# Layer 3 of a four-layer convolution stack: ScalarE's copy of a block moved ahead of the work of the block before it

## The chip, the cores and the metric

The kernel runs on one NeuronCore of a Trainium2 chip. The time is the device time of one launch in microseconds, told as the median of several runs. A profile is one more execution, with its own time. PE is TensorE (matrix products into PSUM), ACT is ScalarE, DVE is VectorE, POOL is GpSimd, SP issues DMAs. Each engine works through its own queue in order; semaphores join them.

## The reference

The input x is 8 images of 128 channels, 56 x 56, float32. Four layers follow, each x = x + f(groupnorm(x)): a window attention, a recurrent network over the pixels, a mixed 3x3 and 1x1 convolution, and, as layer 3, a residual block of two 3x3 convolutions. The change is all in layer 3:

```python
def _L3_conv_ref(x, w1, w2, gamma1, beta1, mean1, var1, gamma2, beta2, mean2, var2):
    residual = x
    out = _conv3x3(x, w1, stride=1)
    out = jax.nn.relu(_bn(out, gamma1, beta1, mean1, var1))
    out = _conv3x3(out, w2, stride=1)
    out = _bn(out, gamma2, beta2, mean2, var2)
    return jax.nn.relu(out + residual)
...
x = x + _L3_conv_ref(_gn(x), ...)
```

## The kernel before

Channels lie on the 128 partitions; X holds all images in SBUF. In layer 3 each 3x3 convolution is computed along the rows in a transformed form: four output pixels of a row come from six sums of the input pixels, multiplied by six transformed weight columns, times three row offsets. An image is cut into 4 blocks of 14 rows (RB = 14, H4 = 14 groups of four pixels in a row, 196 positions). Per image there are two phases: blocks pc3a_0 to pc3a_3 (called a_0 to a_3 here) for the first convolution, reading va, and pc3b_0 to pc3b_3 (b_0 to b_3) for the second, reading vb.

The steps of a block:

- products() (L1440): 18 matrix products on TensorE, 36 records in the profile, into three PSUM banks, m[0], m[1], m[2]. There are six banks, so two blocks can be open. A bank is free again once its readers are done.
- outputs(): ACT copies m[0] to SBUF as c (L1452). DVE makes the sum s and difference d of c and m[1] (L1453, L1454), then w and two rows of the result y (L1456 to L1459), then, after what `between` puts there, the other two rows with m[2] (L1461). s, d, w and y have one buffer each, c two.
- a phase: six() (L1302, L1304, L1305) on ACT applies the batch norm and relu and writes y into `edge`, six planes with the neighbours at the row ends. column_sums() turns `edge` into the sums of vb in three parts: outer() on POOL (ce at L1415, fg at L1416), inner() on DVE (ab at L1420, two planes at L1421 and L1422), ends() on DVE (four planes, L1426 to L1428).
- b phase: ACT applies the second batch norm to y, giving u (L1540). Then normal3() on ACT normalizes a block of the next image into `pad` (L1302 to L1305 again, through six()), and column_sums() makes its sums of va; here POOL does L1421 and L1422 of inner(). residual() on DVE adds the normalized and the raw x (L1553, L1554), and SP issues the store of the block (L1555). u has two buffers.

The order on PE, ACT, DVE and POOL is the order of the program text, set by hand. Two lists hold work for a later place: `middle` is run between the rows of y of the next block, `waiting` after its y. In the kernel before, a block is in ACT's queue: copy, then six() or u and normal3() of this same block; then comes the copy of the next block. In the b phase DVE's place for inner() of the next image is `between`; ends() and then the residual come after y.

A block b_i needs the rows of vb that a_i and a_(i+1) make, since the third row offset reaches two rows into the next block; a_i needs va of blocks up to i only. The first image has more in it: statistics and norm of the seven other images (stats3(), Rest), and va made at its beginning (into_va with "begin").

Of the kernel before, what the change touches and what calls it, by code (L numbers as in the profile page):

```python
# [10 lines left out]
F32 = mybir.dt.float32  # L11
I32 = mybir.dt.int32
U32 = mybir.dt.uint32
AF = mybir.ActivationFunctionType
# [30 lines left out]
def conv_stack_kernel(ctx: ExitStack, tc: tile.TileContext, a: dict, out: bass.AP):  # L45
# [1027 lines left out]
    def convolutions(held=None):  # L1073

        with ExitStack() as l2:
# [246 lines left out]
            with ExitStack() as order:  # L1322
                if held is not None:
                    order.enter_context(tc.manual_schedule(engines={ET.PE, ET.Activation, ET.DVE, ET.Pool}))
                for i in range(NBLK):
                    norms[0].stats(i)
                warm(8, ps_g, "pg")
                norms[0].mean_mm()
                norms[0].mean_end()
                norms[0].var_mm()  # L1330
                warm(26, ps_g, "pg")
                norms[1].stats(0)
                norms[0].root()
                for c in range(5):
                    norms[0].normal([c])
                    spread(0, c)
                nc.vector.tensor_mul(w1, w1, m1)
                nc.vector.tensor_reduce(bsum, bmat, AX.X, ALU.add)
                for i in range(1, NBLK):
                    norms[1].stats(i)  # L1340
                for n in range(B * NBLK):
                    b, i = divmod(n, NBLK)
                    if i == 0 and b + 2 <= B:
                        norms.append(Norm((b + 2) % B, f"l2_{b + 2}"))
                    then = norms[b + 1]
# [36 lines left out]
                    if i == 0 and b in (1, 3):  # L1382
                        weights.append(transformed(f"w{(b + 1) // 2}c_t"))
                    if 1 <= b <= 4 and i >= 3:
                        for f in weights[-1][1][i - 3 + 4 * ((b - 1) % 2) :][:1]:
                            f()
# [56 lines left out]
                            )  # L1443
                return pc

            def outputs(m, name, between):

                shape = [P, 2, RB * H4]
                c, s, d, w = (
                    blk.tile(shape, F32, name=f"{k}_{name}", tag=k, bufs=1 + (k == "c")) for k in ("c", "s", "d", "w")  # L1450
                )
                nc.scalar.copy(c, m[0])  # L1452
                nc.vector.tensor_tensor(s, c, m[1], ALU.add)  # L1453
# [7 lines left out]
                nc.vector.tensor_tensor(at[:, 0:4:3], w, m[2], ALU.add)  # L1461
                return at
# [26 lines left out]

            waiting, middle = [], []

            def settle(fs):
                for f in fs:
                    f()
                fs.clear()

            def layer3(b, begin):  # L1500
                more = b + 1 < B
                rest = Rest() if b == 0 else None
                for i in range(NB):
                    name = f"pc3a_{b}_{i}"
                    pc = products(ua, va, i, name)
                    if rest and i == 2:
                        rest.mean_mm()
                    if rest and i == 3:
                        rest.var_mm()
                    if i in begin:  # L1510
                        settle(middle)
                        settle(waiting)
                        begin[i]()
                    y = outputs(pc, name, lambda: settle(middle))
                    mid = edges[i % 2]
                    six(mid, y, AF.Relu, bn[0][1], bn[0][0])
                    settle(waiting)
                    outer, inner, ends = column_sums(vb, 1 + i * RB, mid, name)
                    outer()
                    middle.append(inner)  # L1520
                    waiting.append(ends)
                    if rest:
                        for k in {0: range(4), 1: range(4, NBLK)}.get(i, ()):
                            stats3(B - 1, k)
                        if i == 2:
                            rest.mean_end()
                        if i == 3:
                            rest.root()
                for i in range(NB):
                    name = f"pc3b_{b}_{i}"  # L1530
                    pc = products(ub, vb, i, name)
                    if i == 0:

                        ends = waiting.pop()
                        settle(waiting)
                        settle(middle)
                        middle.append(ends)
                    y = outputs(pc, name, lambda: settle(middle))
                    u = blk.tile([P, RB * H4, 4], F32, name=f"u_{name}", tag="u")
                    nc.scalar.activation(  # L1540
                        u, y.rearrange("p k x -> p x k"), AF.Identity, bias=shs[:, b : b + 1], scale=bn[1][0]
                    )
                    settle(waiting)
                    if more:
                        normal3(b + 1, i)
                        outer, inner, ends = into_va(f"va_{b}", i, nc.gpsimd)
                        outer()
                        middle.append(inner)
                        waiting.append(ends)
                    flat, cols = u.rearrange("p x k -> p (x k)"), slice(i * RB * HW, (i + 1) * RB * HW)  # L1550

                    def residual(flat=flat, cols=cols):
                        nc.vector.scalar_tensor_tensor(flat, X[:, b, cols], rs[:, b : b + 1], flat, ALU.mult, ALU.add)  # L1553
                        nc.vector.scalar_tensor_tensor(flat, flat, 0.0, X[:, b, cols], ALU.max, ALU.add)  # L1554
                        nc.sync.dma_start(out[b][:, cols], flat)  # L1555

                    waiting.append(residual)

            with ExitStack() as order:
                if held is not None:  # L1560
                    order.enter_context(tc.manual_schedule(engines={ET.PE, ET.Activation, ET.DVE, ET.Pool}))
                for k in range(2):
                    for f in into_va("begin", k, nc.vector, True):
                        f()
                    normal3(0, k + 2)
                begin = {k - 2: lambda k=k: [f() for f in into_va("begin", k)] for k in (2, 3)}
                for b in range(B):
                    layer3(b, {} if b else begin)
                settle(waiting)

    convolutions(held)

# [226 lines left out]
```

## Time and profile before

| | |
|---|---|
| median of the runs | 3569.07 us (3568.85 to 3573.68, three runs) |
| the profiled execution's time | 3572.46 us |
| its span, first to last instruction | 3570.7 us |
| mean granted TensorE clock | 0.985 |
| PE busy | 3421.3 us (96%) |
| DVE busy | 1909.5 us (53%) |
| ACT busy | 1770.0 us (50%) |
| POOL busy | 1393.5 us (39%) |
| layer 3, from its first matrix product at 3073.17 us to the end | 497.5 us |
| one image of layer 3 | 61.2 us |

Shares over the whole span say little here, since the four layers have different limits; layer 3 is the last seventh. A line of the timeline gives start, duration, engine, line, operation, output and inputs with their sizes, and in brackets how long the engine had been idle and what released it. Neighbouring instructions of one engine overlap a little at their ends, so a chain is summed by their starts. A windows row gives the length of the stretch and each engine's busy time in it with its number of instructions, then the granted clock and the DMA share.

### The profile page before, as it was taken

The numbers are of one execution on the slowest core, as the hardware profiler recorded it, in microseconds if no ns is written. First come the engines' busy times: TensorE is split into PE (matmuls) and PEld (weight loads), VectorE is DVE, ScalarE is ACT, GpSimd is POOL, SyncE is SP. The second block draws the span as 40 slices with busy tenths as digits, with TensorE's granted clock in tenths as the row PEclk, the third lists the DMA queues.
The fourth block names the chain that finished last, engine by engine and source line by source line (L and its number), as shares of the span: only waits on it lengthen the run. The fifth ranks groups of instructions, "written<-read, shape, count | busy, mean of one in ns | idle before, by whom it ended". The sixth has DMA issues, their size and how long they took to land.

```text
span 3570.7 us, 87785 instructions
## 1 busy us (share of the span) xinstructions
PE 3421.3 (96%) x30960; PEld 2827.2 (79%) x30960; DVE 1909.5 (53%) x4105; ACT 1770.0 (50%) x5321; POOL 1393.5 (39%) x3774
## 2 busy tenths in 40 slices
PE   8999999999999989999999999999999999988887
PEld 5666666666666669999999999999999943688886
DVE  6888888888787663222111111111122257787787
ACT  5888888888788872222222222222211144454544
POOL 4777777777766651111111111111000056333332
PEclk9999999999999999999999999999999999999999
DMA  5444444444444431111000000000012156100000
GB/s 147 125 123 120 120 125 116 123 116 124 112 112 111 115 89 57 47 45 48 1 1 1 1 1 1 1 1 1 1 51 60 54 144 180 44 32 24 32 23 38
DMA packets 197663, 238.19 MB, mean 67 GB/s; under 512 B 42736, under 2 KB 150128, under 8 KB 197216
## 3 DMA queue, kind: packets, MB, share of 16 engines
q0 software_dynamic: 34624, 117.03, 12.4%
q1 hardware_dynamic: 161760, 115.12, 11.6%
q8 instruction: 250, 4.10, 0.5%
q14 instruction: 197, 1.61, 0.2%
q10 hardware_dynamic: 832, 0.33, 0.0%
HBM read 133.80 MB, written 67.56 MB: 56 GB/s over the span
## 4 chain that ended last, share of the span: by engine, by line
PE 71%; DVE 12%; ACT 6%; issue 6%; DMA 3%; POOL 1%; SPq 1%; POOLq 0%; ACTq 0%; DVEq 0%
PE ps L968 33%; PE pt L539 7%; PE po L1003 5%; PE s L504 5%; PE pc L1194 4%; PE plep L410 4%; PE po L566 3%; PE pi L943 2%; DMA vs<-vpix 2%; DVE nmax L512 2%; ACT e L516 2%; ACT pad L1302 1%; PE pc L1202 1%; PE pvt L296 1%; PE pc3a L1440 1%
## 5 line engine op out<-in xcount | busy, mean ns | idle before, releaser
L968 PE MATMUL ps<-hs,w_gates 128*128 128x136 f32 x7680 | 932.9, 280 | 0.4 <-DVE gk L980 0.4
L968 PEld LDWEIGHTS ps<-hs,w_gates 128*128 128x128 f32 x7680 | 911.1, 190 | 8.6 <-issue 0.6
L516 ACT ACTIVATE e<-s,nmax 128x256 f32<-128x256 f32 x1568 | 728.3, 483 | 199.1 <-DVE nmax L512 199.0
L991 ACT ACTIVATE hs<-ps,bg 128x136 f32<-128x136 f32 x744 | 237.4, 370 | 933.5 <-PE ps L968 926.0
L946 DVE SCALAR_TENSOR_TENSOR inp<-pi,bine,th 128x272 f32<-128x272 f32 x186 | 84.7, 497 | 888.7 <-ACT th L945 888.7
L512 DVE TENSOR_REDUCE nmax<-s 128x2 f32<-128x512 f32 x784 | 507.5, 681 | 43.2 <-PE s L504 42.6
L539 PEld LDWEIGHTS pt<-ident,e 128*128 128x128 f32 x3136 | 352.0, 142 | 130.0 <-issue 50.3
L539 PE MATMUL pt<-ident,e 128*128 128x128 f32 x3136 | 433.7, 281 | 5.4 <-ACT e L516 3.7
L932 POOL TENSOR_TENSOR xn<-X,ctr 128x136 f32<-128x136 f32 (+1 forms) x186 | 96.3, 536 | 875.3 <-PE pi L943 871.3
L968 PEld LDWEIGHTS ps<-inp,w_gates 128*128 128x128 f32 x2976 | 370.2, 190 | 13.5 <-PE pi L943 1.1
L968 PE MATMUL ps<-inp,w_gates 128*128 128x136 f32 x2976 | 375.3, 279 | 0.7 <-DVE inp L946 0.7
L544 DVE COPY eT<-pt 128x512 f32<-128x512 f32 x392 | 267.5, 682 | 149.7 <-PE pt L539 149.7
L516 ACT ACTIVATION_READ_ACCUMULATOR e<-s,nmax 128x1 f32 x1568 | 331.5, 211 | 0.0
L474 POOL COPY ks<-kT 128x64 f32 x1568 | 297.5, 233 | 26.9 <-ACT vrow L302 23.6
L527 POOL TENSOR_TENSOR rc<-rden,own 128x128 f32<-128x128 f32 x392 | 147.7, 396 | 353.0 <-DVE rden L524 199.2
L1440 PE MATMUL pc3a<-va,u_w1c_t 128*128 128x196 f32 x1152 | 217.5, 352 | 39.3 <-ACT c_pc3b L1452 18.6
L566 PE MATMUL po<-eT,vs 128*32 128x128 f32 x6272 | 224.5, 277 | 27.7 <-DMA vs<-vpix 18.1
L544 ACT COPY eT<-pt 128x512 f32<-128x512 f32 x392 | 231.4, 590 | 37.6 <-PE pt L539 37.3
L1440 PEld LDWEIGHTS pc3a<-va,u_w1c_t 128*128 128x128 f32 x1152 | 209.5, 205 | 47.5 <-POOL ce_va L1415 37.9
L504 PE MATMUL s<-ks,qm 32*128 32x256 f32 x3136 | 246.1, 403 | 0.0
L566 PEld LDWEIGHTS po<-eT,vs 128*32 128x32 f32 x6272 | 160.3, 109 | 98.8 <-issue 49.8
L1440 PE MATMUL pc3b<-vb,u_w2c_t 128*128 128x196 f32 x1152 | 202.5, 336 | 21.9 <-DVE vb L1421 14.7
(283 smaller groups left out, 4690.0 us busy)
## 6 DMA issues: line engine op xcount, KB each, us to landing
vs<-vpix SPq DMA_DIRECT2D x1568, 32.0 KB, 2.8
v<-vimg POOLq DMA_DIRECT2D x56, 290.0 KB, 4.1
v<-vimg POOLq DMA_DIRECT2D x56, 289.5 KB, 5.0
v<-vimg POOLq DMA_DIRECT2D x56, 289.0 KB, 5.9
kept<-gk SPq DMA_DIRECT2D x56, 272.0 KB, 2.1
g<-kept SPq DMA_DIRECT2D x56, 272.0 KB, 2.7
xkeep<-X POOLq DMA_DIRECT2D x56, 224.0 KB, 2.4
out_dram<-u_pc3b SPq DMA_DIRECT2D x32, 392.0 KB, 2.4
```

Source lines behind the costliest of these rows:

```text
L474: nc.gpsimd.tensor_copy(kw[:, t : t + 1, :], ks[b][:, bass.ds(at, 1), :])
L504: nc.tensor.matmul(s_["s"][g][:, o, :], w["qm"][h].rearrange("p h x -> p (h x)"), w["kw"][h], start=True, stop=True,)
L512: nc.vector.tensor_reduce(s_["nmax"][:, g, :], s_["s"][g], AX.X, ALU.max, negate=True)
L516: nc.scalar.activation(wins[2 * p + o]["e"][:, g, :], s_["s"][g][:, o, :], AF.Exp, bias=s_["nmax"][:, g, o : o + 1], accum_out=s_["den"][: ...
L527: nc.gpsimd.tensor_tensor(pairs[p]["r"][:, o], rden[:, o].rearrange("p (g c) -> p g c", c=1).broadcast_to((P, 4, CL)), own.rearrange("p (g ...
L539: nc.tensor.transpose(s_["pt"][c][:, g, :], s_["e"][:, g, c * P : (c + 1) * P], ident)
L544: (nc.scalar.copy if c else nc.vector.tensor_copy)(s_["eT"][c], s_["pt"][c])
L566: nc.tensor.matmul(po[ch, o, 0], s_["vw"][:, c, ch], s_["eT"][c][:, g, :], start=(c == 1), stop=(c == 0),)
L968: nc.tensor.matmul(ps[f][:, i], w, src, start=(i == 0 and k == 0 and h != fresh), stop=(k == KH - 1 if h else k == KI - 1 and (s < WARM or ...
L991: nc.scalar.activation(hs[f][:, s % 2, i], ps[f][:, i], AF.Tanh, bias=bg[:, m : m + 1])
L1003: nc.tensor.matmul(po, wout[:, k, :], hs[k // 2][:, :, k % 2], start=(k == 0), stop=(k == KH - 1))
L1440: nc.tensor.matmul(bank[:, half].rearrange("p (y x) -> p y x", x=H4), u[:, dy, k, :], v[:, k, i * RB + dy : i * RB + dy + RB, :], start=(d ...
```

## The change

- outputs() loses the copy; copied() takes it, and block() puts a block's copy right behind its products, ahead of `behind`, a new list.
- What ACT did with y of a block (six() and column sums in the a phase; u, normal3() and column sums in the b phase) becomes a function in `behind`, run in the next block after that block's copy. POOL's outer() moves with it.
- DVE: in the a phase inner() and ends() keep their places. In the b phase the order after y is now residual, inner(), ends(), where inner() stood ahead of the last rows of y.
- In the first image, POOL's and DVE's shares of the first column sums are issued in the order inner, outer, ends; the last statistics of image 6 come after them. Rest.root goes to `behind`.
- The last block of the last image is done in two halves, u, residual and store each; the second half's store is issued by ACT.

```diff
-                    if b >= 2:
+                    if b >= 2 and n + 1 < B * NBLK:
                         stats3(b - 1, i)
...
+            def copied(m, name):
+                c = blk.tile([P, 2, RB * H4], F32, name=f"c_{name}", tag="c")
+                nc.scalar.copy(c, m[0])
+                return c
+
+            def outputs(m, c, name, between):
...
-                nc.scalar.copy(c, m[0])
...
+            def block(u, v, i, name, small=lambda: None, first=None):
+                m = products(u, v, i, name)
+                small()
+                c = copied(m, name)
+                settle(behind)
+                if first:
+                    settle(middle)
+                    settle(waiting)
+                    first()
+                y = outputs(m, c, name, lambda: settle(middle))
+                settle(waiting)
+                return y
...
+                    y = block(ua, va, i, name, small or (lambda: None), begin.get(i))
+
+                    def relu(i=i, y=y, name=name):
+                        mid = edges[i % 2]
+                        six(mid, y, AF.Relu, bn[0][1], bn[0][0])
+                        outer, inner, ends = column_sums(vb, 1 + i * RB, mid, name)
+                        outer()
+                        middle.append(inner)
+                        waiting.append(ends)
+
+                    behind.append(relu)
...
+                        if i == 3:
+                            behind.append(rest.root)
...
+                    y = block(ub, vb, i, name)
+
+                    def affine(i=i, y=y, name=name):
+                        u = blk.tile([P, RB * H4, 4], F32, name=f"u_{name}", tag="u")
+                        flat, cols = u.rearrange("p x k -> p (x k)"), slice(i * RB * HW, (i + 1) * RB * HW)
+
+                        n = 1 if more or i + 1 < NB else 2
+
+                        def part(h):
+                            x = slice(h * (RB * H4 // n), (h + 1) * (RB * H4 // n))
+                            nc.scalar.activation(
+                                u[:, x], y[:, :, x].rearrange("p k x -> p x k"), AF.Identity,
+                                bias=shs[:, b : b + 1], scale=bn[1][0],
+                            )
+
+                        def residual(h):
+                            w = flat.shape[1] // n
+                            f, x = flat[:, h * w : (h + 1) * w], X[:, b, cols][:, h * w : (h + 1) * w]
+                            nc.vector.scalar_tensor_tensor(f, x, rs[:, b : b + 1], f, ALU.mult, ALU.add)
+                            nc.vector.scalar_tensor_tensor(f, f, 0.0, x, ALU.max, ALU.add)
+                            (nc.sync, nc.scalar)[h].dma_start(out[b][:, cols][:, h * w : (h + 1) * w], f)
+
+                        for h in range(n):
+                            part(h)
+                            waiting.append(lambda h=h: residual(h))
+                        if more:
+                            normal3(b + 1, i)
+                            outer, inner, ends = into_va(f"va_{b}", i, nc.gpsimd)
+                            outer()
+                            waiting.extend((inner, ends))
+
+                    behind.append(affine)
...
                 for k in range(2):
-                    for f in into_va("begin", k, nc.vector, True):
+                    outer, inner, ends = into_va("begin", k, nc.vector, True)
+                    for f in (inner, outer, ends):
                         f()
                     normal3(0, k + 2)
+                stats3(B - 2, NBLK - 1)
...
-                settle(waiting)
+                for fs in (behind, middle, waiting):
+                    settle(fs)
```

More of the change, by code (lines that the diff above doesn't have):

```diff
@@ L1444, in products @@
                 return pc
[L1446 to L1450, printed above, removed]
+            def copied(m, name):
[3 more added lines that the diff above has]
+            def outputs(m, c, name, between):
+                s, d, w = (
+                    blk.tile([P, 2, RB * H4], F32, name=f"{k}_{name}", tag=k, bufs=1) for k in ("s", "d", "w")
                 )
-                nc.scalar.copy(c, m[0])
                 nc.vector.tensor_tensor(s, c, m[1], ALU.add)
@@ L1488, in into_va @@
                 return column_sums(va, CUT[k], part3(k), f"{name}_{k}", *how)
-            waiting, middle = [], []
+            behind, middle, waiting = [], [], []
             def settle(fs):
@@ L1498, in settle @@
                 fs.clear()
+            def block(u, v, i, name, small=lambda: None, first=None):
[10 more added lines that the diff above has]
+                return y
             def layer3(b, begin):
-                more = b + 1 < B
-                rest = Rest() if b == 0 else None
+                more, rest = b + 1 < B, Rest()
                 for i in range(NB):
                     name = f"pc3a_{b}_{i}"
[L1505 to L1511, printed above, removed]
-                        settle(waiting)
[L1513 to L1522, printed above, removed]
+                    small = {2: rest.mean_mm, 3: rest.var_mm}.get(i) if b == 0 else None
+                    y = block(ua, va, i, name, small or (lambda: None), begin.get(i))
[7 more added lines that the diff above has]
+                    behind.append(relu)
+                    if b == 0:
                         for k in {0: range(4), 1: range(4, NBLK)}.get(i, ()):
@@ L1527, in layer3 @@
                         if i == 3:
-                            rest.root()
+                            behind.append(rest.root)
                 for i in range(NB):
                     name = f"pc3b_{b}_{i}"
[L1531 to L1557, printed above, removed]
+                    y = block(ub, vb, i, name)
@@ L1568, in convolutions @@
                     layer3(b, {} if b else begin)
-                settle(waiting)
+                for fs in (behind, middle, waiting):
+                    settle(fs)
     convolutions(held)
```

## The prediction

> **What bounds the kernel now.** I read the stage windows first. Layer 3 runs from about 3073 us to the end, and its images repeat every 61.2 us.
>
> ```profile
> core 0: us, PE busy (x) PEld busy (x) DVE busy (x) ACT busy (x) POOL busy (x), PEclk, DMA share, GB/s
> 3104.33:3128.46 24.13, 24.13 (x146) 23.83 (x145) 17.25 (x46) 11.54 (x13) 5.62 (x7) 1.00 0.00 1
> ...
> 3207.43:3268.67 61.24, 54.25 (x288) 52.57 (x289) 48.34 (x113) 29.42 (x36) 21.95 (x25) 0.92 0.07 27
> ...
> 3452.30:3513.58 61.28, 51.66 (x288) 49.06 (x289) 48.41 (x113) 29.39 (x36) 22.01 (x25) 0.97 0.07 27
> ```
>
> The first row is four blocks of 36 matmul records with PE never waiting: 24.13 / 4 = 6.03 us a block, 48.3 us for the eight blocks of an image. PE's busy of 51.7 to 54.3 in whole images is the same work, partly at a lower granted clock (last columns). DVE is busy 48.3 of 61.2 us. Neither is full, so a loop between engines sets the period. The waits of six images show where:
>
> ```profile
> DVE s_pc3b L1453 <- ACT c_pc3b L1452: 50.8, 18, 5.3
> ...
> DVE s_pc3a L1453 <- ACT c_pc3a L1452: 26.0, 19, 1.5
> ```
>
> DVE waits (50.8 + 26.0) / 6 = 12.8 us an image for L1452's copy, and that copy stands behind other ACT work (ACT's timeline, then DVE's):
>
> ```profile
> 3308.21 1.79 ACT L1540 ACTIVATE u_pc3b<-y_pc3b,shs,bns 128x784 f32<-128x784 f32 x1 [3.17 <-DVE y_pc3b L1461]
> 3309.91 1.83 ACT L1302 ACTIVATE pad<-X,offs,rs 128x784 f32<-128x784 f32 x1
> 3311.64 0.70 ACT L1304 ACTIVATE pad<-X,offs,rs 128x182 f32<-128x182 f32 x1
> 3312.25 0.70 ACT L1305 ACTIVATE pad<-X,offs,rs 128x182 f32<-128x182 f32 x1
> 3312.86 0.46 ACT L1452 COPY c_pc3b<-pc3b 128x392 f32<-128x392 f32 x1
> ```
>
> ```profile
> 3313.34 0.56 DVE L1453 TENSOR_TENSOR s_pc3b<-c_pc3b,pc3b 128x392 f32<-128x392 f32 x1 [1.53 <-ACT c_pc3b L1452]
> ```
>
> Block n's result y frees ACT; ACT does u(n) and the three normalizations, 4.65 us, and only then copies block n+1, though PE already runs a block further on. That loop is 4.65 + 0.48 + DVE's s..y: 8.3 us a block.
>
> **Part 1: the copy ahead.** The copy now stands before the work of the block before it. In the b phase TensorE stands two blocks ahead (at 3305.09 it starts the block whose banks copy b_1 had just freed, that is b_3), so copy b_2 could have run some 7.9 us before 3312.86. The 12.8 us of DVE waits go. Behind the copy in ACT's queue now stand six()/u/normal3 of the previous block, and POOL's ce/fg and DVE's sums behind those; where TensorE is late, they wait with it, for its first pair (36/3 records, 2.0 us) and the copy (0.46). TensorE itself needs none of these within two blocks, so I cost this at 0 in steady state; if the lead were lost it is up to 2.5 us a block. The tile y has one buffer: L1458 of block n+1 overwrites what six(n) reads. After a late copy six (1.9 us) runs against s, d, w, w (1.5), a wait of 0 to 0.4 us; when DVE is the late engine ends() or the residual precede them, so 0.
>
> **Part 2: what DVE must do.** Start to start, L1453 and L1454 take 0.95, L1456 to L1459 1.09, L1461 0.48: outputs() 2.51. inner() in the a phase is 1.14 (L1420 to L1422), ends() 1.09, the residual 2.0, ab of the next image's block 0.5. An image: 8 x 2.51 + 4 x (1.14 + 1.09) + 4 x (2.0 + 0.5 + 1.09) = 43.4 us. The page's 48.3 has nearly 5 more, lost against POOL:
>
> ```profile
> 3272.93 1.78 DVE L1553 SCALAR_TENSOR_TENSOR u_pc3b<-X,rs,u_pc3b 128x784 f32<-128x784 f32 x1
> 3274.74 1.67 DVE L1554 SCALAR_TENSOR_TENSOR u_pc3b<-u_pc3b,X 128x784 f32<-128x784 f32 x1
> ```
>
> ```profile
> 3272.82 1.06 POOL L1415 TENSOR_TENSOR ce_pc3a<-edge 128x392 f32<-128x392 f32 x1 [0.54 <-ACT edge L1302]
> 3273.84 1.74 POOL L1416 TENSOR_TENSOR fg_pc3a<-edge 128x392 f32<-128x392 f32 x1
> ```
>
> Elsewhere the first two take 1.02 and 0.98, and L1416 1.02. Here they take turns: ce to 3273.88, the first residual to 3274.71, fg to 3275.58, the second to 3276.41. s, d and L1461 read PSUM and run beside POOL at their usual 0.56. [...] An average reading of today's rows (5 us lost an image, whatever the order) would leave DVE at 48.4; by the turns I have to place each POOL instruction. [...] ACT's offsets are today's: after y, ce of the a phase can start at 1.2, fg at 2.2; of the b phase at 3.7 and 4.9.
>
> With DVE never waiting, from one y to the next:
> - a_1 to a_2, a_2 to a_3, a_3 to b_0: ends 1.09; s, d to 2.04, covering ce; the first w to 2.47, fg to 3.4; the other three to 4.2, inner to 5.35, y 5.8. Three times: 17.5.
> - b_0 to b_1: ends, s..y, POOL idle: 3.6.
> - b_1 to b_2: first residual 1.0, ce of b_0 to 1.95, second residual 2.85, fg 3.8, ab 4.3; L1426 twice with L1421/L1422 between, 5.8; L1427 6.1, ce of b_1 7.05, L1428 7.3; s, d 8.25, covering fg; w..y 9.8.
> - b_2 to b_3: residual 2.0, ab 2.5, L1426 with POOL's two to 4.0, L1427 4.25, ce 5.2, L1428 5.5, s, d 6.45 over fg, w..y 8.0. b_3 to a_0: 7.9, its tiles being smaller.
> - a_0 to a_1: the same with inner, 9.1. Here ce/fg of a_0 stand in POOL's queue behind L1421/L1422 of the sums that moved back.
>
> Sum 17.5 + 3.6 + 9.8 + 8.0 + 7.9 + 9.1 = **55.9 us**, of which 12.5 is POOL's. Bounds: TensorE's 48.3 below; 43.4 + all of POOL's 18.8 = 62.2 above. The sums moving behind y and the residual cost no instruction; the next image's va(i) is needed by TensorE only at a_i, at least two blocks later. The output DMAs stay in SP's order; their issue follows each residual as now, 2.4 us to land, while u's two buffers come round in over 11.
>
> TensorE at 48.3 has 7.6 us to spare. **The clock** can eat it: after the 1.94 us gap at 3266.7 the clock granted around 3271 was 0.50, and that block's 36 records took 7.67 us rather than 6.03. [...]
>
> **Part 3: begin, and the last store.** DVE is continuously busy up to the first b phase, so moving stats3 and ce there moves no sum: PE starts earlier without use, 0 +- 1.5. Up to the first y of a b phase 1.1 us goes, because ends() of a_3 now follows it. The ends:
>
> ```profile
> 3115.57 0.55 DVE L1461 TENSOR_TENSOR y_pc3b<-w_pc3b,pc3b 128x392 f32<-128x392 f32 x1
> ```
>
> ```profile
> 3544.20 0.55 DVE L1461 TENSOR_TENSOR y_pc3b<-w_pc3b,pc3b 128x392 f32<-128x392 f32 x1
> ...
> 3563.76 0.97 DVE L1554 SCALAR_TENSOR_TENSOR u_pc3b<-u_pc3b,X 128x784 f32<-128x784 f32 x1
> ```
>
> Seven periods lie between: 428.6 / 7 = 61.2. From the last b_0's y to DVE's end today is 20.0 us, with one 4.4 us wait for an output DMA to free u. After: y of b_1 at 3.6, b_2 at 8.1, b_3 at 13.0 (TensorE's b_3 ends at 12.4), then u's halves wait for u to come free (10.1 + 4.4 = 14.5), ACT's first half to 15.4, residual halves to 17.4. That is 2.6 less, and half a transfer last, by my estimate 0.6 less (bounds 0 and half of 2.4): 3.2.
>
> **Sum.** 1.1 + 7 x (61.2 - 55.9) + 3.2 = 41.5 us off the profiled execution, 3572.46 us (span 3570.7): 3531. The median of the runs, 3569.07, is 3.4 lower: **3527.5**.
>
> **Rivals.**
> - *DVE waits turn into POOL turns (above)*, 60%: 3527.5, own range 3512 (period 54) to 3545 (58.5).
> - *The turns mostly miss each other*, since each one shifts the next: the loss stays near today's 5 us, DVE 48.4 and TensorE 48.3 meet at about 50 with their coupling. 1.1 + 7 x 11.2 + 3.2 = 82.7: 3486. 30%. For it: s, d and y, 1.43 us of each block, hide POOL wholly.
> - *The clock*: every block gets a gap and runs at a_0's 7.67. 8 x 7.67 = 61.4, plus the 3.3 us stall: 64.7, 7 x 3.5 - 4.3 = +20: 3589, slower. It decides from a mean block of 7.4. For it: the 0.50 above; against: clock 1.00 in b blocks that follow gaps of 0.4. 5%.
> - *No effect*: the copy ahead still waits for its matmuls, period 61.2, only the ends gain 4.3: 3565. Against: TensorE's two-block lead. 5%. The upper bound 62.2 of the turns comes out here too: 3572.
>
> The range takes most of the first two cases: 3486 up to 3550 (leaving out some of the second, the third and fourth). About 0.2% (7 us) can be told from no change; faster 0.90, same 0.05, slower 0.05.
>
> **What would show it.** Right: waits of L1453 on L1452 nearly gone; windows of about 56 us with DVE over 95% busy; L1427/L1428, L1456 and L1553 lengthened by up to 0.95, POOL's L1416 too; TensorE with several us of waits on L1421/L1426 or on banks. DVE near 48 busy with a period near 50 is the second case; a clock under 0.8 through the stage the third; copies that ACT waits for on PE the fourth.

## The result, and the profile after

The kernel after takes **3513.94 us** (median of four runs, 3505.71 to 3514.93); before, measured beside it, 3568.96 us (four runs, 3564.27 to 3573.68). The ratio is 0.984, with a 95% interval of 0.9824 to 0.9857. The profiled execution took 3514.11 us, with a span of 3512.3 us.

The period, from the y of one b_0 to the y of the next, is 53.63 us (mean of seven) where it was 61.23. The stage windows of the kernel after, one image each, with the columns named in their first line:

```profile
core 0: us, PE busy (x) PEld busy (x) DVE busy (x) ACT busy (x) POOL busy (x), PEclk, DMA share, GB/s
3221.97:3275.60 53.63, 50.48 (x300) 49.25 (x299) 53.35 (x113) 29.48 (x36) 22.85 (x24) 1.00 0.08 31
3275.60:3329.23 53.63, 49.33 (x290) 47.52 (x289) 53.35 (x113) 29.45 (x36) 22.96 (x24) 1.00 0.08 31
```

DVE is busy for 53.35 of 53.63 us, so DVE should set the period; the experiments test this. Its own work is the 43.4 us that the prediction added up; the other 10 us are spent inside its instructions. The granted clock is 1.00 in these two images and 0.97 in some others. (TensorE's work is 288 records an image throughout. The windows begin and end at different points of it, so they hold 280 to 306 records, and PE busy lies between 49.3 and 51.2 us.)

The waits of layer 3 in the kernel after, over six and a half images (engine, line and what it waited for; then us in total, how often, the longest):

```profile
ACT edge L1302 <- DVE y_pc3a L1464: 105.9, 27, 6.3
...
ACT u_pc3b L1550 <- issue: 27.9, 11, 2.7
...
PE pc3b L1440 <- DVE vb L1421: 14.3, 7, 2.0
...
ACT c_pc3b L1448 <- PE pc3b L1440: 3.1, 4, 1.0
```

No wait of DVE is in that list. Where s waited 12.8 us an image for c, ACT now waits for DVE's y, POOL waits mostly for DVE and ACT, and TensorE's one long wait is 2.0 us an image on DVE's L1421. The copy waits for TensorE in four blocks of the stretch, at most 1.0 us. ACT's timeline in a b phase shows how far ahead the copy now runs:

```profile
3281.36 1.80 ACT L1550 ACTIVATE u_pc3b<-y_pc3b,shs,bns 128x784 f32<-128x784 f32 x1
3283.06 1.82 ACT L1302 ACTIVATE pad<-X,offs,rs 128x784 f32<-128x784 f32 x1
3284.79 0.71 ACT L1304 ACTIVATE pad<-X,offs,rs 128x182 f32<-128x182 f32 x1
3285.40 0.71 ACT L1305 ACTIVATE pad<-X,offs,rs 128x182 f32<-128x182 f32 x1
3286.02 0.46 ACT L1448 COPY c_pc3b<-pc3b 128x392 f32<-128x392 f32 x1
3289.17 1.80 ACT L1550 ACTIVATE u_pc3b<-y_pc3b,shs,bns 128x784 f32<-128x784 f32 x1 [2.69 <-issue]
```

DVE's timeline from b_2 to b_3 shows who reads that copy, and when:

```profile
3289.01 1.02 DVE L1558 SCALAR_TENSOR_TENSOR u_pc3b<-X,rs,u_pc3b 128x784 f32<-128x784 f32 x1
3290.07 0.98 DVE L1559 SCALAR_TENSOR_TENSOR u_pc3b<-u_pc3b,X 128x784 f32<-128x784 f32 x1
3290.96 0.56 DVE L1420 SCALAR_TENSOR_TENSOR ab_va<-pad 128x392 f32<-128x392 f32 x1
3291.44 0.97 DVE L1426 SCALAR_TENSOR_TENSOR va<-ce_va 128x196 f32<-128x196 f32 x2
3292.33 0.68 DVE L1427 SCALAR_TENSOR_TENSOR va<-fg_va,ce_va 128x196 f32<-128x196 f32 x1
3292.94 1.18 DVE L1428 SCALAR_TENSOR_TENSOR va<-ce_va,fg_va 128x196 f32<-128x196 f32 x1
3294.04 0.55 DVE L1456 TENSOR_TENSOR s_pc3b<-c_pc3b,pc3b 128x392 f32<-128x392 f32 x1
```

The copy was done at 3286.48; s reads it at 3294.04, when DVE comes to it. DVE runs without a gap, but three of the lines are long. Undisturbed, L1426 (two instructions), L1427 and L1428 take 0.63, 0.35 and 0.35. POOL's timeline in the same stretch says why:

```profile
3291.66 0.53 POOL L1421 TENSOR_TENSOR va<-ab_va 128x196 f32<-128x196 f32 x1 [4.20 <-PE pc3a L1440]
3292.15 0.65 POOL L1422 TENSOR_TENSOR va<-ab_va 128x196 f32<-128x196 f32 x1
3292.78 1.12 POOL L1415 TENSOR_TENSOR ce_va<-pad 128x392 f32<-128x392 f32 x1
3294.07 1.02 POOL L1416 TENSOR_TENSOR fg_va<-pad 128x392 f32<-128x392 f32 x1 [0.18 <-ACT pad L1305]
```

L1421 and L1422 fall among L1426 and L1427, and ce (L1415) goes ahead of L1428, whose end waits for it. fg (L1416) falls under s and d, which read PSUM and keep their 0.55: it costs nothing.

In time order, the 58.4 us between the two spans (3570.7 less 3512.3) are 0.9 up to the first y of a b phase, 7 x (61.23 - 53.63) = 53.2 in the seven periods, and 4.3 in the tail, from the end of the last b_0's y to the end of the span (25.95 before, 21.65 after). DVE's timeline of the kernel after at these points:

```profile
3114.70 0.56 DVE L1464 TENSOR_TENSOR y_pc3b<-w_pc3b,pc3b 128x392 f32<-128x392 f32 x1
...
3490.10 0.56 DVE L1464 TENSOR_TENSOR y_pc3b<-w_pc3b,pc3b 128x392 f32<-128x392 f32 x1
...
3506.85 0.57 DVE L1559 SCALAR_TENSOR_TENSOR u_pc3b<-u_pc3b,X 128x392 f32<-128x392 f32 x1
```

### The profile page after: what moved, and what is told of

Read it like the earlier page. It is cut to its first block, busy times and chain, and to the rows that moved or that the text cites. A ratio compares the mean times of both kernels' runs of the same rounds, so it can differ in the third digit from the quotient of the medians.

```text
span 3512.3 us, 87799 instructions
## 1 busy us (share of the span) xinstructions
PE 3396.8 (97%) x30960; PEld 2810.4 (80%) x30960; DVE 1943.8 (55%) x4107; ACT 1772.1 (50%) x5322; POOL 1399.9 (40%) x3774
## 3 DMA queue, kind: packets, MB, share of 16 engines
q14 instruction: 197, 1.61, 0.2%
## 4 chain that ended last, share of the span: by engine, by line
PE 74%; DVE 14%; issue 4%; DMA 4%; ACT 2%; SPq 1%; POOL 1%; POOLq 0%; DVEq 0%; ACTq 0%
PE ps L968 33%; PE pt L539 7%; PE po L1003 5%; PE s L504 5%; PE plep L410 4%; PE pc L1194 4%; PE po L566 3%; DMA vs<-vpix 3%; PE pc3b L1440 3%; PE pi L943 2%; DVE nmax L512 2%; SPq L487 1%; PE pc L1202 1%; PE pvt L296 1%; DVE eT L544 1%
## 5 line engine op out<-in xcount | busy, mean ns | idle before, releaser
L1440 PE MATMUL pc3a<-va,u_w1c_t 128*128 128x196 f32 x1152 | 203.5, 335 | 13.9 <-DVE d_pc3a L1457 5.8
L1440 PEld LDWEIGHTS pc3a<-va,u_w1c_t 128*128 128x128 f32 x1152 | 194.6, 193 | 22.0 <-POOL fg_pc3a L1416 5.4
```

Source lines behind the costliest of these rows:

```text
L1440: nc.tensor.matmul(bank[:, half].rearrange("p (y x) -> p y x", x=H4), u[:, dy, k, :], v[:, k, i * RB + dy : i * RB + dy + RB, :], start=(d ...
```

## The experiments

The question is what the 53.63 us consist of. My theory: DVE's own work plus its turns with POOL, taken where both read SBUF. The rivals: the copy's place did nothing and the moved sums did all; TensorE, or its coupling with DVE, sets 53.6; or DVE loses its time to something other than POOL. Layer 2 ends at a different time in each execution (its last addition on DVE starts between 3059.34 and 3071.15 us in the profiles here), which blurs totals by several us. So kernels are compared by the period, which is read inside layer 3, and by the tail; the whole time is given beside them. A stretch is the time from one block's y to the next one's. Diffs are against the kernel after.

### The copy alone, and the sums alone

**copy_late** puts the copy back behind the previous block's work and leaves the rest of the change:

```diff
                 small()
-                c = copied(m, name)
                 settle(behind)
...
                     first()
+                c = copied(m, name)
                 y = outputs(m, c, name, lambda: settle(middle))
```

> The changed kernel with the copy put back behind the work of the block before it; the order on DVE (residual, then sums) and the ends stay as changed. My theory: the loop ACT work, copy, s..y is back. A b-phase block costs 4.65 + 0.48 + 2.6 = 7.75 us (not 8.3, since ab no longer stands between the rows of y), b_0 to b_1 rises from 3.6 to 7.75, a-phase blocks are 6.1, a_0 to a_1 about 8.0: 57.3 us an image against 53.6, DVE's waits on L1448 are back at about 8 us an image, total about 3540. Rival (the copy's place is the whole change): 61.2 an image, 3567. Rival (the copy's place is nothing, the moved sums are all): 53.6, 3514.

3548.58 us (3542.95 to 3552.74), ratio 0.9921 (0.9904 to 0.9938); period **58.10**, tail 23.58. The period is 0.8 longer than I expected, 0.5 of it from a_0 to a_1 (8.54 in place of about 8.0). DVE waits for the copy again (waits of that kernel from 3200 to 3300 us, 1.7 periods):

```profile
DVE s_pc3b L1456 <- ACT c_pc3b L1448: 11.2, 5, 4.2
...
DVE s_pc3a L1456 <- ACT c_pc3a L1448: 5.1, 4, 1.3
```

**sums_between** leaves the copy ahead and puts the b phase's inner() back between the rows of y, and the residual back to the end:

```diff
                         def part(h):
...
-                            waiting.append(lambda h=h: residual(h))
                         if more:
...
-                            waiting.extend((inner, ends))
+                            middle.append(inner)
+                            waiting.append(ends)
+                        for h in range(n):
+                            waiting.append(lambda h=h: residual(h))
```

> The changed kernel with the next image's sums back in their old place: inner() between the rows of y, ends() before the residual. Copy ahead as changed. My theory: DVE's work is the same and POOL's turns cost nearly the same (its two planes partly under the last rows of y, 0.35 to 0.5 us in place of 0.68; ce or fg still meets one run of two-input work, 0.83 to 1.1), 53.3 to 54 us an image, 3512 to 3517. Rival (moving the sums matters): 1 us an image or more either way, under 3507 or over 3521.

3518.86 us (3517.69 to 3521.37), ratio 0.984 (0.9823 to 0.9856); period **54.14**, just outside what I expected. The stretch b_0 to b_1 is 4.74 instead of 3.61, since ab (0.5) now stands there and waits for the normalization of b_0 (3.4 us in six images); the others together are 0.6 shorter.

The two kernels, with before and after, make a square of periods:

| | sums and residual in their old places | moved back |
|---|---|---|
| copy behind the block's work | 61.23 (before) | 58.10 |
| copy ahead | 54.14 | 53.63 (after) |

With the old order of the sums, the copy ahead is worth 7.1 us an image, with the new one 4.5; moving the sums is worth 3.1 alone and 0.5 once the copy is ahead. The rival that gives all to the sums falls. (In before, ends() of a_3 also stands ahead of the last rows of b_0's y; its part in the 3.1 wasn't separated.)

### What POOL costs DVE

**no_pool** gives all of POOL's work in the steady state to DVE: two switches put ce and fg at the head of ends(), and va's two planes go into inner() on DVE.

```diff
-                    other.tensor_tensor(ce, img[:, 3:5], img[:, 1:3], ALU.subtract)
-                    nc.gpsimd.tensor_tensor(fg, img[:, 0:4:3], img[:, 2:6:3], ALU.subtract)
+                    if not ce_late:
+                        other.tensor_tensor(ce, img[:, 3:5], img[:, 1:3], ALU.subtract)
+                    if not (fg_late or fg_in):
+                        nc.gpsimd.tensor_tensor(fg, img[:, 0:4:3], img[:, 2:6:3], ALU.subtract)
...
                 def ends():
+                    if ce_late:
+                        nc.vector.tensor_tensor(ce, img[:, 3:5], img[:, 1:3], ALU.subtract)
+                    if fg_late:
+                        nc.vector.tensor_tensor(fg, img[:, 0:4:3], img[:, 2:6:3], ALU.subtract)
...
-                        outer, inner, ends = column_sums(vb, 1 + i * RB, mid, name)
+                        outer, inner, ends = column_sums(vb, 1 + i * RB, mid, name, ce_late=True, fg_late=True)
...
-                            outer, inner, ends = into_va(f"va_{b}", i, nc.gpsimd)
+                            outer, inner, ends = into_va(f"va_{b}", i, ce_late=True, fg_late=True)
```

> The changed kernel with all of POOL's work in the steady state of layer 3 (ce, fg, and L1421/L1422 of the next image) given to DVE, ce and fg at the head of ends(). My theory (DVE sets the period, and loses to POOL, turn by turn, about as long as POOL's work would take it itself): DVE's own 43.4 + 16 x 0.48 + 8 x 0.28 = 53.3 us an image, as before, 3512. Rival (POOL's work is nearly free, and the 10 us that DVE's instructions are longer have another cause): 53.6 + 9.9 = 63.5 an image, 3583.

One run, 3516.76 us; period **53.44**. Its window (columns as above) has POOL at nothing, 23 more instructions on DVE, and the same time:

```profile
3227.00:3280.00 53.00, 50.25 (x294) 49.78 (x293) 52.59 (x136) 29.48 (x36) 0.00 (x0) 0.97 0.08 31
```

DVE's own work rises by sixteen instructions of 0.47 and eight of 0.28 us from start to start, 9.8 in all: 43.4 + 9.8 = 53.2. So what POOL takes off DVE, DVE pays again in turns. The help is worth nothing in this loop: the period without it is 0.2 us shorter.

**pool_writes** lets POOL fill ce and fg with zeros in place of the differences; the output lacks these sums. POOL then writes as many tiles but reads none for them.

```diff
-                    other.tensor_tensor(ce, img[:, 3:5], img[:, 1:3], ALU.subtract)
-                    nc.gpsimd.tensor_tensor(fg, img[:, 0:4:3], img[:, 2:6:3], ALU.subtract)
+                    if quick:
+                        nc.vector.tensor_tensor(ce, img[:, 3:5], img[:, 1:3], ALU.subtract)
+                    else:
+                        nc.gpsimd.memset(ce, 0.0)
+                    nc.gpsimd.memset(fg, 0.0)
```

> The changed kernel with ce and fg only filled with zeros by POOL (no reading), so the sums of columns are left out of the computation; DVE, ACT and TensorE do all that they did. My theory (turns at the SBUF reads): DVE falls to 43.4 + 4 x 0.68 = 46.1 us an image, TensorE becomes the bound with its 48.3 and its stall of 2 before b_0: 48.6 to 50.3 an image, 3479 to 3491. Rival (no matter what POOL reads): 53.6 and 3514.

One run, 3473.35 us; period **47.76** (six of the seven; the first is 46.53). The window of that kernel:

```profile
3227.00:3280.00 53.00, 53.00 (x322) 53.00 (x321) 51.00 (x126) 33.74 (x42) 12.45 (x28) 1.00 0.10 39
```

Now TensorE is full and DVE waits for it at s (10.3 us from 3130 to 3440). This is TensorE's floor, 47.76 / 8 = 5.97 us a block, a little under my 6.03. The period is also under the 48.6 to 50.3 that I expected: the stall before b_0, which I had added, doesn't occur. DVE's a stretches that aren't waiting are 4.75 us (ends() at 3239.76, then at 3244.51), as its own instructions add up. A DVE and a POOL line of that kernel show that a POOL instruction that only writes (0.42 us) takes no turn here; L1431 there is L1428 of the kernel after, with two inputs in SBUF, and keeps its usual 0.34 under it:

```profile
3235.85 0.34 DVE L1431 SCALAR_TENSOR_TENSOR va<-ce_va,fg_va 128x182 f32<-128x182 f32 x1
```

```profile
3235.67 0.42 POOL L1418 MEMSET ce_pc3a<- 128x392 f32 x1
3236.03 0.42 POOL L1419 MEMSET fg_pc3a<- 128x392 f32 x1
```

### TensorE's share

**pe_more** issues one pair of products of each b_2 twice, 12 more records an image, some 2 us more for TensorE. The result stays the same: the first product of each half starts its sum anew, so the repeat overwrites a sum with itself.

```diff
+                    again = 2 if v is vb and i == 2 and pair[0] == 0 else 1
...
-                    for half, k in enumerate(pair):
+                    for half, k in [h for h in enumerate(pair) for _ in range(again)]:
```

> The changed kernel with the last pair of products of each b_2 done twice: 12 more records an image, 2.0 us of TensorE, the same result. My theory (DVE sets the period, TensorE has 5 us to spare): 53.6 us an image, 3514. Rival (TensorE's stalls count): 55.6 us an image, 3528.

One run, 3511.71 us; period **53.64**. In its window TensorE takes in the 12 records and the length stays:

```profile
3212.00:3265.60 53.60, 51.67 (x312) 51.31 (x311) 53.32 (x113) 29.72 (x36) 22.87 (x24) 1.00 0.08 31
```

TensorE has at least 2 us an image to spare, so neither its work nor its coupling with DVE sets 53.6.

### The ends

**ends_undone** undoes the third part of the change: the last block whole, the first column sums in the order outer, inner, ends, and the last statistics in their old place.

```diff
-                    if b >= 2 and n + 1 < B * NBLK:
+                    if b >= 2:
...
-                        n = 1 if more or i + 1 < NB else 2
+                        n = 1
...
-                    for f in (inner, outer, ends):
+                    for f in (outer, inner, ends):
...
-                stats3(B - 2, NBLK - 1)
```

> The changed kernel with its ends as before: the last block whole, its store by SP alone; the first column sums in the old order and the last statistics of image 6 in their old place. My theory: 53.6 us an image unchanged; from the last b_0's y to the end 22.4 to 22.8 us in place of 21.65 (the transfer is whole again; DVE ends when it did), the stretch from layer 2's last addition to the first b_0's y within 1 us of the changed kernel's 47.9. Total 3514 to 3516. Rival (the halves carry the gain at the end): 24.5 to 26 at the end.

One run, 3514.53 us; period 53.63, tail **23.00**, just above the 22.4 to 22.8 that I expected. The halves are worth 23.00 - 21.65 = 1.35 us, so 2.95 of the tail's 4.3 come from the first two parts. This is good to about half a us: the tails of sums_between and fg_a, which keep the halves, are 21.4 and 22.2.

From layer 2's last addition to the first y of a b phase it takes 46.89 us, against 47.93 in the kernel after and 47.19 before. This difference of 1.0 us is not shown to be the new order's. With the new order s of a_0 does start 1.0 us later (13.47 us after that addition, 12.48 with the old one), but by y of a_1 this is made up (26.72 and 26.74). What is left arises behind a_2, and there executions of the same order differ by as much: sums_between, whose program is that of the kernel after up to this y, takes 46.80. The traces show TensorE's pace there. After TensorE's wait before a_3 the granted clock is 0.50 for 6.83 us in the kernel after (3094.99 to 3101.82), where a_3's 36 records take 8.82 us and s of a_3 waits 1.8 us for TensorE; they take 7.90 us in sums_between and 7.89 in ends_undone.

### Fewer turns

If turns set the period, then taking the right POOL instructions away should shorten it. Three kernels move work from POOL to DVE.

**hybrid** moves seven instructions that take turns with DVE, fg of a_1 to a_3 and ce in the b phase; ce of the a phase, fg of a_0 and of the b phase, and va's two planes stay on POOL. POOL's own lines have the same switches as in no_pool:

```diff
                 def inner():
...
+                    if fg_in:
+                        nc.vector.tensor_tensor(fg, img[:, 0:4:3], img[:, 2:6:3], ALU.subtract)
...
                 def ends():
+                    if ce_late:
+                        nc.vector.tensor_tensor(ce, img[:, 3:5], img[:, 1:3], ALU.subtract)
...
-                        outer, inner, ends = column_sums(vb, 1 + i * RB, mid, name)
+                        outer, inner, ends = column_sums(vb, 1 + i * RB, mid, name, fg_in=i > 0)
...
-                            outer, inner, ends = into_va(f"va_{b}", i, nc.gpsimd)
+                            outer, inner, ends = into_va(f"va_{b}", i, nc.gpsimd, ce_late=True)
```

> The changed kernel with those of POOL's instructions given to DVE that meet two-input work: in the a phase fg of blocks 1 to 3 (made behind inner()), in the b phase ce (at the head of ends()); the others stay on POOL, where s and d cover them. My theory: a DVE instruction of 0.48 in place of a turn of 0.85 or more. The three a-phase stretches 5.2 in place of 5.71, b_1 to b_2 8.1 in place of 9.33, the next two 7.3, a_0 to a_1 9.0: 51.0 us an image, 7 x 2.6 = 18 us off the changed kernel: 3496. Rival (DVE's work counts and POOL's does not): 53.6 + 7 x 0.48 = 57 an image, 3538. Rival (TensorE with its stall before b_0 is met first): 52.5 to 53.6, 3506 to 3514.

3513.87 us (3505.87 to 3522.41), ratio 0.9851 (0.9838 to 0.9865); period **53.24**, a miss. The a stretches came nearly as expected (5.30 to 5.37), and so did b_3 to a_0 (7.30); b_1 to b_2 (8.97), b_2 to b_3 (7.53) and a_0 to a_1 (9.80) did not. The period lies in the range of the rival that has TensorE first, but that isn't the cause: in the waits of this kernel (3130 to 3480 us) DVE has no row. Without ce, POOL starts fg and the next tiles at other times, and these meet DVE instructions that the old ones missed. DVE's timeline of that kernel; L1467 is the first w, which was free before, and L1435 and L1436 are L1427 and L1428 of the kernel after:

```profile
3277.65 1.07 DVE L1467 TENSOR_TENSOR w_pc3b<-s_pc3b 128x196 f32<-128x196 f32 x1
...
3298.76 1.16 DVE L1435 SCALAR_TENSOR_TENSOR va<-fg_va,ce_va 128x182 f32<-128x182 f32 x1
...
3299.84 1.15 DVE L1436 SCALAR_TENSOR_TENSOR va<-ce_va,fg_va 128x182 f32<-128x182 f32 x1
```

In the stretches b_1 to a_0, ce's turn went and DVE's own ce (0.47) came, but fg now met the first w (1.07 us here, undisturbed 0.35; 0.70 in the next block). The stretch a_0 to a_1 is longer than the 8.53 of the kernel after, since both ce and fg of a_0 now meet DVE's last two sums.

**fg_a** keeps only the a phase's half of it: the diff above without `ce_late`.

> The changed kernel with only fg of a_1, a_2 and a_3 given to DVE (behind inner()); the b phase as changed. My theory: three stretches of 5.36 in place of 5.71, all others unchanged: 52.6 us an image, 7.4 us off the changed kernel's steady part, 3507. Rival (turns form again elsewhere, as when ce of the b phase went to DVE as well): 53.0 to 53.7, 3510 to 3514.

**3509.25 us** (3508.66 to 3509.49), ratio 0.9821 (0.9804 to 0.9837); period **52.60**, as expected to the last digit. The a stretches fell from 5.71 to 5.37 and no other stretch moved. In the kernel after, fg and the second w of an a block (L1460) met like this, first DVE's timeline and then POOL's:

```profile
3260.98 0.50 DVE L1459 TENSOR_TENSOR w_pc3a<-s_pc3a 128x196 f32<-128x196 f32 x1
3261.41 1.17 DVE L1460 SCALAR_TENSOR_TENSOR w_pc3a<-d_pc3a 128x196 f32<-128x196 f32 x1
```

```profile
3261.22 1.13 POOL L1416 TENSOR_TENSOR fg_pc3a<-edge 128x392 f32<-128x392 f32 x1
```

In fg_a DVE does fg itself, and the second w (L1468 there) is short again; its timeline:

```profile
3260.11 0.50 DVE L1467 TENSOR_TENSOR w_pc3a<-s_pc3a 128x196 f32<-128x196 f32 x1
3260.54 0.35 DVE L1468 SCALAR_TENSOR_TENSOR w_pc3a<-d_pc3a 128x196 f32<-128x196 f32 x1
...
3262.50 0.56 DVE L1426 TENSOR_TENSOR fg_pc3a<-edge 128x392 f32<-128x392 f32 x1
```

A turn of 0.81 us goes, and 0.47 of work comes: 0.34 a block, 1.03 an image. Over seven periods that is 7.2 us; its tail is 0.6 longer (22.25). The medians of the two kernels, 3509.25 and 3513.94, stand in this order, but their intervals against before overlap; it is the period that separates them. fg_a is the fastest kernel here with the whole output.

**fit** goes further: fg on DVE everywhere (in the b phase behind s and d of the next block, with L1427 and L1428), va's two planes on DVE, and a_0's ce on DVE as well.

```diff
+                    if fg_end:
+                        late.append(rest)
...
+                settle(late)
...
-                        outer, inner, ends = column_sums(vb, 1 + i * RB, mid, name)
+                        outer, inner, ends = column_sums(vb, 1 + i * RB, mid, name, ce_late=i == 0, fg_in=True)
...
-                            outer, inner, ends = into_va(f"va_{b}", i, nc.gpsimd)
+                            outer, inner, ends = into_va(f"va_{b}", i, fg_end=True)
```

> The changed kernel with POOL left only the ce's that s and d can cover: fg everywhere, the two planes of va, and ce of a_0 on DVE; in the b phase the last two planes (L1427, L1428) with their fg come behind s and d of the next block. My theory: a-phase stretches 5.36 (the first 5.84), b_0 to b_1 3.6, b_1 to b_2 8.0, the next two 7.15, a_0 to a_1 8.8: 51.2 us an image, 17 us off: 3497. Rival (a turn is met again in each b stretch): 7.6 there, 53 an image, 3510.

3518.21 us (3511.85 to 3519.81), ratio 0.9843 (0.9827 to 0.9858); period **53.44**, a miss again. From b_1 to b_2 (9.01, expected 8.0) two turns are left: ce of two blocks meets the second residual (1.74 us instead of 0.98) and DVE's own fg (1.39 instead of 0.58). From b_2 to a_0 hardly a turn is left, but DVE does the work, and the stretches (7.37, 7.30) are little shorter than the 7.55 and 7.49 of the kernel after. And a_0's ce on DVE made ends() 0.5 us longer, so that a_1's ce on POOL, which s and d used to cover, met L1438 (L1428 of the kernel after); the stretch a_1 to a_2 became 6.64 where I had 5.84. The two lines of that kernel, DVE and POOL:

```profile
3313.46 1.18 DVE L1438 SCALAR_TENSOR_TENSOR vb<-ce_pc3a,fg_pc3a 128x196 f32<-128x196 f32 x1
```

```profile
3313.34 1.08 POOL L1416 TENSOR_TENSOR ce_pc3a<-edge 128x392 f32<-128x392 f32 x1 [12.73 <-ACT edge L1302]
```

## Why the prediction was right, and where its steps were off

The forecast was 3527.5 us with a range of 3486 to 3550; the median is 3513.94. The likeliest case was the one that happened: the waits for the copy turned into turns with POOL, and DVE sets the period. Its period of 55.9 was 2.3 too long. Against the profiled execution I was 3531 - 3514.1 = 16.9 us too high, and 7 x 2.27 = 15.9 of it are the period. The case's own range, 3512 to 3545, just holds the result. The whole range also covers most of the second case, in which the turns miss each other, so the total alone would not have told the two apart; the period and the kernels without POOL's readings do.

- **Part 1, the waits go.** Right: none is left in the list of waits, and putting the copy back brings them back (copy_late). That TensorE's lead covers the copy is right as well.
- **Part 2, DVE's own work, 43.4 us.** Right, by three kernels: the stretch without a turn, b_0 to b_1, took 3.61 (predicted 3.6); without ce and fg an a stretch is 4.75; and with all of POOL's work added no_pool comes to 53.44 where the sum gives 53.2.
- **Part 2, the turns, 12.5 us. This is the term that was mis-sized**: 53.63 - 43.4 = 10.2. They are where I placed them, and each is cheaper. The 12.5, and the 18.8 of the upper bound (16 x 0.95 + 8 x 0.45), rest on 0.95 for each ce and fg and 0.45 for each of L1421 and L1422 on POOL; no run shows DVE losing that much to one of them. L1421 and L1422 on POOL delay DVE by 0.34 each: in the stretch shown above L1426 takes 0.89 from start to start instead of 0.55, and L1427 0.61 instead of 0.27. ce ahead of L1428 costs 0.83, fg ahead of L1460 0.81. For ce and fg I had taken the price from a single place of the trace of before, the two residuals, and there I counted how long POOL works (0.95, net of its waiting) and not how much longer DVE took. The rows of that place give less: the first residual takes 3274.74 - 3272.93 = 1.81 us from start to start, undisturbed 1.06, so 0.75. The coupling is the one foretold; the price of a turn was about 0.1 us too high. Stretch by stretch, predicted and measured:

| | b_0 to b_1 | b_1 to b_2 | b_2 to b_3 | b_3 to a_0 | a_0 to a_1 | a_1 to b_0 (three) |
|---|---|---|---|---|---|---|
| predicted | 3.6 | 9.8 | 8.0 | 7.9 | 9.1 | 17.5 |
| measured | 3.61 | 9.33 | 7.55 | 7.49 | 8.53 | 17.13 |

- **The clock step: the row was right that a gap of 2 us can halve the clock; in the kernel after it did in three of seven images.** In before a gap of 1.94 us was followed by a granted clock of 0.50, and the block behind it took 7.67 us instead of 6.03. The kernel after has one such gap in each image, before b_0, of 2.04 to 2.05 us; the 3.3 us that the rival "the clock" adds for this stall were my estimate, and the kernel after doesn't show them. TensorE's timeline after it, in two images:

```profile
3210.41 25.16 PE L1440 MATMUL pc3b<-vb,u_w2c_t 128*128 128x196 f32 x140 [2.04 <-DVE vb L1421]
...
3264.04 23.51 PE L1440 MATMUL pc3b<-vb,u_w2c_t 128*128 128x196 f32 x140 [2.05 <-DVE vb L1421]
```

Windows at the two places (columns as above), first two around the first gap, then two around the second:

```profile
3207.63:3211.04 3.41, 1.37 (x9) 1.07 (x8) 3.38 (x9) 0.07 (x1) 1.09 (x1) 1.00 0.00 0
3211.04:3214.45 3.41, 3.41 (x12) 3.41 (x11) 3.41 (x9) 2.27 (x4) 2.10 (x2) 0.50 0.03 7
...
3262.24:3265.65 3.41, 1.61 (x9) 1.55 (x10) 3.38 (x11) 0.82 (x1) 0.11 (x1) 1.00 0.01 2
3265.65:3269.06 3.41, 3.41 (x23) 3.41 (x22) 3.41 (x8) 1.45 (x4) 2.11 (x2) 1.00 0.00 0
```

The same gap is followed by half the clock in one image and by full speed in the other; of the seven such gaps three have it. What differs is how the gap lies in time. In the traces of before and after, every change of the granted clock lies on a grid of 3.41 us, and the windows above are laid on that of the kernel after. The first gap falls whole into one step of the grid, which leaves TensorE idle for 3.41 - 1.37 = 2.04 us of that step. The second gap is cut by an edge, and its larger part is 3.41 - 1.61 = 1.80 us. From 3100 us on, counted over these two traces in steps at full clock, each of the 16 with 1.93 us or more without a matrix product was followed by half the clock, and none of the 217 with 1.89 us or less; of the three with 1.92 us two were. The half clock costs 25.16 - 23.51 = 1.65 us, nearly half of one step. An image loses 0 or 1.65 us of TensorE's time. DVE, with TensorE 2 us or more below it, covers that: the periods are 53.63 with and without it.

- **Part 3, the start: predicted 1.1 + 0 earlier.** Not shown either way. The first y is 0.87 earlier in the profiles, but layer 2 ended 1.61 earlier there; counted from its last addition, y is 0.74 later (47.93 against 47.19), and executions of the same program differ by more than that (47.93 and 46.80, see ends_undone). That TensorE starts earlier without use was right: 4.17 us after the addition instead of 4.80. That DVE is continuously busy up to there was not: in the trace of before it waits 0.37 us at s of a_2 and 1.09 us for the square root of the other images' variances.
- **Part 3, the tail: predicted 3.2, measured 4.3.** The steps were good: from y of the last b_0, b_1 to b_3 came at 3.61, 8.07 and 12.53 (predicted 3.6, 8.1, 13.0), and DVE's end at 17.3 (predicted 17.4). But I set 17.4, counted from that y's start, against today's 20.0, counted from its end. From the end it is 16.8, so 3.2 and not 2.6. The last store lands 1.1 sooner after DVE's end (4.9 against 6.0), where I estimated 0.6.
- **The rivals.** "The turns mostly miss each other" fails by DVE's busy time of 53.35 and by no_pool and pool_writes; its loss of 5 us is 10. TensorE's floor of 48.3 is nearly confirmed (47.76), but is reached only when POOL no longer reads for ce and fg. "The clock" and "no effect" are out by the windows and the waits.

## What to carry to other kernels

In this loop a helper engine that reads SBUF wasn't free for DVE, though DVE never waited for it (a period of 53.63 us with POOL's work and 53.44 with DVE doing it): before counting work moved to POOL as saved, compare what it costs DVE in turns with what DVE would need itself (here 0.83 against 0.47 us for the same two-input difference), and look for places like s and d here, which read PSUM and kept their 0.55 us under POOL's fg. When instructions were moved, others met that had missed each other (in hybrid the first w took 1.07 us instead of 0.35); the only kernel of three whose period I could foretell was the one that left all other start times in place. And when a wait is removed, add up the next engine's own work by start-to-start times from a stretch without disturbance: that sum (43.4) held in the three kernels that could show it, while a busy time (48.3) already had the losses in it.

## What the runs showed of the hardware

- A GpSimd difference of 128x392 float32 takes 1.02 us alone and costs DVE 0.71 to 0.83 us when it goes ahead of a DVE instruction with two inputs in SBUF (0.71 and 0.75 at the residuals of before, 0.81 at L1460 and 0.83 at L1428 of the kernel after). At the residuals of before they end in turns, ce at 3273.88, the first residual at 3274.71, fg at 3275.58 and the second at 3276.41, though the second had no wait before it (it started at 3274.74).
- A GpSimd memset of a tile of that size (0.42 us) costs such a DVE instruction nothing (0.34 us under it in pool_writes), and s, d and y, which have one input in PSUM, keep their 0.55 to 0.56 us under a reading GpSimd (all three in before, s and d in the kernel after).
- A float32 block of 36 records takes 5.97 us with TensorE full. In the traces of before and after the granted clock changes on a grid of 3.41 us: from 3100 us on, each step at full clock with 1.93 us or more without a matrix product (16) was followed by half the clock, and none with 1.89 us or less (217). In the kernel after a gap of 2.04 to 2.05 us was followed by half the clock in three of seven images, where it cost 1.65 us (25.16 against 23.51), and by 1.00 in the others.
